# Transposing features per tile, layer blocks of two tiles and a drifting token stream in a recommendation kernel

## The chip, the cores and the metric

The kernel runs on one core of one Trainium2 chip. A core has a matrix engine (TensorE, "PE" in the profile, with its weight loads listed as "PEld"), a vector engine (VectorE, "DVE"), an activation engine (ScalarE, "ACT"), a general engine (GpSimd, "POOL", which here issues the gathers) and a queue engine (SyncE, "SP"). They run their own instruction streams in order and meet at semaphores. The metric is device microseconds of one execution. The profile is a hardware record of one execution.

## The reference

For each of B = 16384 rows the model looks up embeddings, averages them, runs a three-layer perceptron and adds a "wide" sum:

```python
tok = word_emb[token_idx].mean(axis=1)        # 32 rows of 300 out of 50000
e1 = emb_mh1[mh1_idx].mean(axis=1)            # 20 rows of 64; e2, e3 alike
o1 = emb_oh1[oh1_idx]                         # one row of 64; o2, o3, o4 alike
emb = concatenate([tok, e1, e2, e3, o1, o2, o3, o4], axis=1)      # 748 columns
wide = wide_mh1[mh1_idx].sum(axis=(1, 2)) + ... + wide_oh4[oh4_idx][:, 0]
h = relu(emb @ W1 + b1)                       # 1024
h = relu(h @ W2 + b2)                         # 512
h = relu(h @ W3 + b3)                         # 256
return sigmoid(h @ Wd + bd + wide)
```

All arrays are fp32.

## The kernel before

A tile is 128 rows, so there are 128 tiles. Each tile is worked through in 11 steps (`STEPS`; ten of 6 and one of 4 row pairs), and four kinds of work are interleaved in every step, in one order written out by hand (`manual_schedule`, the loop at L476 to L524):

- **Counts.** The seven small tables are looked up by counting. VectorE builds one-hot matrices for the next step (`one_hots`, "row" and "slice", L294), TensorE multiplies them (12 matmuls per step, "pc", L312), and ScalarE copies the result out as fp8 ("cnt", L319). The PSUM tile "pc" has one buffer and the one-hots have two, so the matmuls of step i wait for the copy of step i-1, and VectorE's one-hots for step i+1 wait for the matmuls of step i-1.
- **Tokens.** POOL gathers rows of the word table (`tokens`, L224): a group is two gathers of 128 rows of 300 values, 16 groups make a tile. VectorE adds a group to a running sum (`add_up`, L211 to L215) three groups after its gathers were written into the program (`TOK_LAG`). The pool of row tiles has 6 buffers, so a gather waits until the group six before it has been added. The `Paced` object spreads the 16 groups over the 11 steps, 1 or 2 per step.
- **Small sums.** The counts of the tile before are multiplied with the tables (`small_sums`, "pg", 138 matmuls per tile, L337) and VectorE reduces the result into the feature tile `g` (L343). When a tile is done, `wide_term` (L351) sums the seven wide columns into a 128x1 tile.
- **Layers.** Four finished tiles form a block of 512 columns. `transposed` (L371) turns their features by 24 TensorE transposes ("pt", L378) into six chunks, each of which VectorE scales into the operand `x` (L379). Then `layer` (L388, L397) does W1, W2 and W3 with 88 matmuls of 512 columns per block, each of which stands as two records in the profile, and ScalarE's relu after each output chunk. The last product ("po", L413) also takes the wide tiles in, by one transposing matmul per tile (L417). `Paced` gives each step a share of this work. The last four tiles are blocks of 2, 1 and 1.

In one step VectorE's order is one-hots, token adds, reduce; TensorE's is pc, pg, layer matmuls. `ps_h` has two PSUM buffers, used in turn for transposes, layer outputs, `po` and the transposed lookup keys. After the last counts, 11 more steps follow, in which only small sums and layers are left.

Of the kernel before, what the change touches and what calls it, by code (L numbers as in the profile page):

```python
# [17 lines left out]
P = 128  # L18
# [5 lines left out]
TOK_LAG = 3  # L24
BLOCK = 512
HALF = P // 2
# [3 lines left out]
CHUNK_WORK = 1  # L30
TABLE_PACE = 1.2
LAYER_TIME = 10
# [6 lines left out]
G_COLS = TOK_D + 7 * ROW  # L39
# [7 lines left out]
def kernel(  # L47
# [23 lines left out]
    NSUB = BLOCK // P  # L71
# [5 lines left out]
    for f in SMALL:  # L77
# [4 lines left out]
    tokp = ctx.enter_context(tc.tile_pool(name="tok", bufs=2 * TOK_LAG))  # L82
    const = ctx.enter_context(tc.tile_pool(name="const", bufs=1))
    idxp = ctx.enter_context(tc.tile_pool(name="idx", bufs=2))
# [4 lines left out]
    gp = ctx.enter_context(tc.tile_pool(name="g", bufs=NSUB + 1))  # L89
    wp = ctx.enter_context(tc.tile_pool(name="wide", bufs=2 * NSUB))  # L90
    xp = ctx.enter_context(tc.tile_pool(name="x", bufs=1))
# [8 lines left out]
        [(0, 128)],  # L100
        [(128, 256)],
        [(256, 300), (684, 748)],
        [(300, 428)],
        [(428, 556)],
        [(556, 684)],
    ]
# [7 lines left out]
    scale = const.tile([P, NK], F32, name="scale")  # L114
    nc.vector.memset(scale, 1.0)
    nc.vector.memset(scale[:, 0:2], 1.0 / N_TOK)
    nc.vector.memset(scale[0 : TOK_D - 256, 2:3], 1.0 / N_TOK)
    nc.vector.memset(scale[:, 3:4], 1.0 / N_MH)
    nc.vector.memset(scale[0:EMB, 4:5], 1.0 / N_MH)
# [25 lines left out]
    def load_tables(part0, tag):  # L145
        raw = xp.tile([P, PART, ROW], F32, name="raw", tag=tag)
        for f in SMALL:
            table, (h0, h1) = tables[f], slices[f]
            full, rest = divmod(table.shape[0], P)
            a, b = max(h0, part0), min(h0 + full, part0 + PART)  # L150
            if a < b:
                nc.sync.dma_start(
                    out=raw[:, a - part0 : b - part0, :],
                    in_=table[(a - h0) * P : (b - h0) * P, :].rearrange("(h p) d -> p h d", p=P),
                )
            if rest and part0 <= h0 + full < part0 + PART:
                nc.vector.memset(raw[:, h0 + full - part0, :], 0.0)
                nc.sync.dma_start(out=raw[0:rest, h0 + full - part0, :], in_=table[full * P :, :])
        return raw
# [44 lines left out]
    under_way = []  # L204
    features = {}

    def add_up(t, q, rows):
# [4 lines left out]
        else:  # L212
            nc.vector.tensor_add(tok_sum, tok_sum, a)  # L213
            to = features[t][:, 0:TOK_D] if q == n_groups - 1 else tok_sum
            nc.vector.tensor_add(to, tok_sum, b)  # L215

    def tokens(t, it):


        for q in range(n_groups):  # L220
            rows = tokp.tile([P, TOK_GROUP * TOK_D], F32, name="tok_rows")
            for r in range(TOK_GROUP):
                j = q * TOK_GROUP + r
                nc.gpsimd.indirect_dma_start(  # L224
                    out=rows[:, r * TOK_D : (r + 1) * TOK_D],
                    out_offset=None,
                    in_=word,
                    in_offset=bass.IndirectOffsetOnAxis(ap=it[:, j : j + 1], axis=0),
                )
            under_way.append((t, q, rows))  # L230
            if len(under_way) > TOK_LAG:
                add_up(*under_way.pop(0))
            yield 1

    def last_tokens():
        for group in under_way:
            add_up(*group)

    def load_indices(blk):
# [15 lines left out]
        return it, ix  # L255
# [71 lines left out]
    def small_sums(g, cnt):  # L327
# [3 lines left out]
        for i in (0, 2, 4, 6):  # L331
# [9 lines left out]
            at = TOK_D + i * ROW  # L341
# [9 lines left out]
    def wide_term(g):  # L351
        wide = wp.tile([P, 1], F32, name="wide")
        at = TOK_D + EMB
        nc.vector.tensor_reduce(
            wide,
            g[:, at : at + 6 * ROW].rearrange("p (c d) -> p c d", d=2 * ROW)[:, :, 0:2],
# [3 lines left out]
        nc.vector.tensor_add(wide, wide, g[:, G_COLS - 1 : G_COLS])  # L360
        return wide

    def chunk(g, k):
        if k < 2:
            return g[:, k * P : (k + 1) * P]
        if k == 2:
            return g[:, 2 * P : TOK_D + EMB]
        at = TOK_D + (1 + 2 * (k - 3)) * ROW + 1
        return g[:, at : at + 2 * EMB]

    def transposed(x, gs):  # L371

        n = len(gs) * P
        for k in range(NK):
            kk = chunk_k[k]
            pt = ps_h.tile([P, BLOCK], F32, name="pt", tag="ph")
            for s, g in enumerate(gs):
                nc.tensor.transpose(pt[:kk, s * P : (s + 1) * P], chunk(g, k), ident)  # L378
            nc.vector.tensor_scalar(  # L379
                x[:kk, k, 0:n], pt[:kk, 0:n], scale[:kk, k : k + 1], None, ALU.mult  # L380
            )
            yield CHUNK_WORK

    def layer(dst, weights, bias, src, kks, n_out, n):
        for m in range(n_out):
            ph = ps_h.tile([P, BLOCK], F32, name="ph", tag="ph")
            for k, kk in enumerate(kks):
                nc.tensor.matmul(  # L388
                    ph[:, 0:n],
                    weights[:kk, k, m * P : (m + 1) * P],  # L390
                    src[:kk, k, 0:n],
                    start=(k == 0),
                    stop=(k == len(kks) - 1),
                )
                if k < len(kks) - 1:
                    yield 1
            nc.scalar.activation(dst[:, m, 0:n], ph[:, 0:n], AF.Relu, bias=bias[:, m : m + 1])  # L397
            yield 1

    def mlp(b0, gs, wides):  # L400

        n = len(wides) * P
        x = xp.tile([P, NK, BLOCK], F32, name="x", tag="even")
        yield from transposed(x, gs)
        h1 = xp.tile([P, M1, BLOCK], F32, name="h1", tag="odd")
        yield from layer(h1, w1_sb, b1_sb, x, chunk_k, M1, n)
        h2 = xp.tile([P, M2, BLOCK], F32, name="h2", tag="even")
        yield from layer(h2, w2_sb, b2_sb, h1, [P] * M1, M2, n)
        h3 = xp.tile([P, M3 + 1, BLOCK], F32, name="h3", tag="odd")
        yield from layer(h3, w3_sb, b3_sb, h2, [P] * M2, M3, n)  # L410
        po = ps_h.tile([1, BLOCK], F32, name="po", tag="ph")
        for k in range(M3):
            nc.tensor.matmul(  # L413
                po[:, 0:n], wd_sb[:, k : k + 1], h3[:, k, 0:n], start=(k == 0), stop=False
            )
        for s, wide in enumerate(wides):
            nc.tensor.matmul(  # L417
                po[:, s * P : (s + 1) * P], wide, ident, start=False, stop=(s == len(wides) - 1)
            )
        y = h3[0:1, M3, 0:n]  # L420
        nc.scalar.activation(y, po[:, 0:n], AF.Sigmoid, bias=bd_sb)
# [3 lines left out]
    class Paced:  # L425


        def __init__(self, gen):
            self.gen, self.done = gen, 0

        def to(self, size):
            while self.done < size:
                work = next(self.gen, None)
                if work is None:
                    return
                self.done += work
# [27 lines left out]

    tiles = B // P
    mlp_time = (NK * (CHUNK_WORK + M1) + M1 * M2 + M2 * M3 + M3) * LAYER_TIME
    ctx.enter_context(tc.manual_schedule())
    sizes = [NSUB] * (tiles // NSUB - 1) + [NSUB - 2, 1, 1]
    it, ix = load_indices(0)
# [5 lines left out]
    gs, wides, layers, before, b0 = [], [], None, None, 0  # L475
    for t in range(tiles + 1):  # L476
        s = t % NSUB
        sums = None
        if before:
            features[t - 1] = g = gp.tile([P, G_COLS], F32, name="g")  # L480
            sums = sums_by_step(small_sums(g, before))
        if t < tiles:
            if s == 0 and t:
                it, sc = next_it, next_sc
            cnt = cp.tile([P, 2, HALF, n_h], FP8, name="cnt", tag="counts")
            toks = Paced(tokens(t, it[:, s, :].bitcast(U32)))
        else:
            last_tokens()
        for i in range(STEPS):
            if t < tiles:  # L490
                hot_now = hot
                if s == 1 and i == 0 and t + NSUB < tiles:
                    next_it, ix = load_indices(t // NSUB + 1)
                if s == 2 and i == 0 and t + NSUB < tiles + 1:
                    next_keys = lookup_keys(ix)
                if i < STEPS - 1:
                    hot = one_hots(sc, s, i + 1)
                elif t + 1 < tiles:
                    hot = one_hots(next_sc if s == NSUB - 1 else sc, (s + 1) % NSUB, 0)
                counts(cnt, hot_now, i)  # L500
                tables_on_chip.to(TABLE_PACE * (t * STEPS + i - 2))
                if t == 1 and i == STEPS - 1:
                    load_weights()
                toks.to(n_groups * (i + 1) / STEPS)
            if s == 2 and i == 1 and t + NSUB < tiles + 1:
                next_sc = key_columns(next_keys)
            done = next(sums) if sums else 0
            if layers:
                share = (n_h + layers_time) * (i + 1) / STEPS - done
                layers.to((layers_before + share) / LAYER_TIME)  # L510
        if layers:
            layers_before += layers_time
        if before:
            assert done == n_h and next(sums, None) is None
            gs.append(g)
            wides.append(wide_term(g))
        before = cnt if t < tiles else None
        if len(gs) == sizes[0]:
            if layers:
                layers.finish()  # L520
# [44 lines left out]
```

## Time and profile before

| | |
|---|---|
| median of 9 runs | 7125.86 us (7106.88 to 7139.03) |
| the profiled execution | 7131.99 us, of which the span of its instructions is 7130.2 us |
| TensorE | 5657.8 us busy (79%), 41320 matmul records, mean granted clock 0.905 |
| VectorE | 3793.0 us (53%) |
| ScalarE | 2461.9 us (35%) |
| POOL | 3882.2 us (54%), 4096 gathers of 948 ns |
| DMA engines | 32.9% of their time on gathers |

Busy shares are averages over the whole span. A line of the groups gives busy time, the mean of one instruction, and after the bar the time for which its engine stood idle just before it, with what released it. "issue" is time in which nothing visible was waited for; "remote" and "another core or an unknown queue" mean that a wait ended without a record that explains it. Matmuls are pipelined: in the timeline, "x18" with 4.08 us is a train of 18, and the pitch of one is smaller than the duration of one.

### The profile page before, as it was taken

The numbers are of one execution on the slowest core, as the hardware profiler recorded it, in microseconds if no ns is written. First come the engines' busy times: TensorE is split into PE (matmuls) and PEld (weight loads), VectorE is DVE, ScalarE is ACT, GpSimd is POOL, SyncE is SP. The second block draws the span as 40 slices with busy tenths as digits, with TensorE's granted clock in tenths as the row PEclk, the third lists the DMA queues.
The fourth block names the chain that finished last, engine by engine and source line by source line (L and its number), as shares of the span: only waits on it lengthen the run. The fifth ranks groups of instructions, "written<-read, shape, count | busy, mean of one in ns | idle before, by whom it ended". The sixth has DMA issues, their size and how long they took to land.

```text
span 7130.2 us, 104252 instructions
## 1 busy us (share of the span) xinstructions
PE 5657.8 (79%) x41320; PEld 3481.0 (49%) x41320; DVE 3793.0 (53%) x8014; ACT 2461.9 (35%) x1938; POOL 3882.2 (54%) x4103
## 2 busy tenths in 40 slices
PE   4688788877877888877878877877878787887889
PEld 3444444544444444444444444444444444444457
DVE  6555555555555555555555555555555555555553
ACT  4333333333333333333333333333333333333332
POOL 6555555555555555555555555555555555555552
PEclk8789998999899998898989999998999999999899
DMA  5333333333333333333333333333333333333331
GB/s 155 93 91 90 94 92 92 92 91 92 90 90 92 91 90 92 92 92 90 90 90 94 91 92 91 91 92 90 89 89 92 91 90 90 93 93 90 91 86 46
DMA packets 252890, 652.60 MB, mean 92 GB/s; under 512 B 119009, under 2 KB 119524, under 8 KB 252399
## 3 DMA queue, kind: packets, MB, share of 16 engines
q0 software_dynamic: 196608, 629.41, 32.9%
q1 hardware_dynamic: 55791, 16.53, 1.0%
q8 instruction: 323, 5.29, 0.3%
q14 instruction: 168, 1.38, 0.1%
HBM read 645.59 MB, written 0.07 MB: 91 GB/s over the span
## 4 chain that ended last, share of the span: by engine, by line
PE 37%; another core or an unknown queue 19%; issue 16%; DVE 16%; POOL 6%; ACT 2%; DMA 2%; DVEq 0%; POOLq 0%; ACTq 0%
PE ph L388 17%; PE pg L337 13%; PE pc L312 6%; POOL tok_rows L224 6%; DVE slice L294 5%; DVE own L213 4%; DVE own L215 3%; DMA tok_rows<-in_word_emb_dram,it 2%; DVE row L294 2%; ACT cnt L319 2%; PE pt L378 1%; DVE g L343 1%; DVE x L379 1%; DVE own L211 0%
## 5 line engine op out<-in xcount | busy, mean ns | idle before, releaser
L224 POOL DMA_INDIRECT tok_rows<-in_word_emb_dram,it x4096 | 3881.3, 948 | 3169.5 <-DVE own L215 1726.8
L319 ACT ACTIVATE cnt<-pc 128x1656 fp8e3<-128x1656 f32 (+1 forms) x1408 | 2122.4, 1507 | 3971.4 <-remote 1931.8
L337 PE MATMUL pg<-terms,cnt 128*128 128x195 bf16 x17664 | 2111.5, 269 | 396.6 <-issue 241.5
L337 PEld LDWEIGHTS <-cnt 128*128 128x128 fp8e3 x17664 | 1745.7, 146 | 630.1 <-issue 490.1
L294 DVE TENSOR_TENSOR row<-own,sc 128x768 bf16<-128x768 bf16 (+1 forms) x1408 | 761.5, 541 | 1900.5 <-remote 1248.5
L312 PE MATMUL pc<-slice,row 64*128 64x138 bf16 x16384 | 804.3, 233 | 1001.3 <-ACT cnt L319 418.9
L388 PE MATMUL ph<-x,w_sb 128*128 128x512 f32 (+5 forms) x3264 | 1569.4, 611 | 25.2 <-issue 23.0
L312 PEld LDWEIGHTS <-row 64*128 64x128 bf16 x16384 | 567.0, 99 | 2010.3 <-issue 1495.0
L388 PE MATMUL ph<-h,w_sb 128*128 128x512 f32 (+2 forms) x2720 | 1337.3, 619 | 32.0 <-issue 30.4
L213 DVE TENSOR_TENSOR own<-own,tok_rows 128x300 f32<-128x300 f32 x1920 | 918.3, 478 | 65.8
L343 DVE TENSOR_REDUCE g<-pg 128x130 f32<-128x390 f32 (+1 forms) x512 | 261.2, 510 | 1208.0 <-remote 579.9
L215 DVE TENSOR_TENSOR own<-own,tok_rows 128x300 f32<-128x300 f32 x1792 | 856.9, 478 | 61.9
L388 PEld LDWEIGHTS ph<-x,w_sb 128*128 128x128 f32 (+1 forms) x3264 | 601.6, 206 | 481.6 <-issue 475.9
L294 DVE TENSOR_TENSOR slice<-own,sc 128x828 bf16<-128x828 bf16 (+1 forms) x1408 | 795.4, 565 | 0.0
L388 PEld LDWEIGHTS ph<-h,w_sb 128*128 128x128 f32 x2720 | 508.1, 210 | 426.6 <-issue 424.7
L397 ACT ACTIVATE h<-ph,b_sb 128x512 f32<-128x512 f32 (+2 forms) x476 | 314.7, 661 | 616.9 <-PE ph L388 329.2
L379 DVE TENSOR_SCALAR x<-pt,scale 128x512 f32<-128x512 f32 (+4 forms) x204 | 138.3, 712 | 49.2 <-PE pt L378 45.2
L378 PE MATMUL pt<-ident,g 128*128 128x128 f32 (+1 forms) x768 | 120.2, 304 | 8.1 <-DVE x L379 7.7
L378 PEld LDWEIGHTS pt<-ident,g 128*128 128x128 f32 (+1 forms) x768 | 101.8, 159 | 12.2 <-DVE x L379 10.6
L211 DVE TENSOR_TENSOR own<-tok_rows 128x300 f32<-128x300 f32 x128 | 61.3, 479 | 4.4
L215 DVE TENSOR_TENSOR g<-own,tok_rows 128x300 f32<-128x300 f32 x128 | 60.2, 470 | 4.4
L413 PE MATMUL po<-h,wd_sb 128*1 128x512 f32 (+2 forms) x136 | 60.9, 566 | 0.3
(34 smaller groups left out, 286.4 us busy)
## 6 DMA issues: line engine op xcount, KB each, us to landing
tok_rows<-in_word_emb_dram,it POOLq DMA_INDIRECT x4096
ix<-in_idx_dram SPq DMA_DIRECT2D x128, 32.0 KB
w_sb<-in_W_dram SPq DMA_DIRECT2D x6, 512.0 KB
raw<-in_mh_dram SPq DMA_DIRECT2D x3, 747.5 KB
it<-in_idx_dram SPq DMA_DIRECT2D x32, 64.0 KB
w_sb<-in_W_dram SPq DMA_DIRECT2D x1, 2048.0 KB
raw<-in_mh_dram SPq DMA_DIRECT2D x1, 617.5 KB
out_dram<-h SPq DMA_DIRECT2D x31, 2.0 KB
```

What stands on the lines that cost most here:

```text
L213: nc.vector.tensor_add(tok_sum, tok_sum, a)
L215: nc.vector.tensor_add(to, tok_sum, b)
L224: nc.gpsimd.indirect_dma_start(out=rows[:, r * TOK_D : (r + 1) * TOK_D], out_offset=None, in_=word, in_offset=bass.IndirectOffsetOnAxis(ap ...
L294: nc.vector.tensor_tensor(one[:, 0:rows, :].rearrange("p i (n d) -> p i n d", d=2), iota[:, 0:n].rearrange("p (n d) -> p n d", d=2).unsque ...
L312: nc.tensor.matmul(pc[:, f, k // n, at : at + n_h], hot[0][half, k, :], hot[1][half, k, :], start=True, stop=True,)
L319: nc.scalar.activation(cnt[:, :, b : b + rows, :].rearrange("l f (g k) h -> l f g (k h)", g=2), pc[:, :, :, 0 : n * n_h], AF.Copy, scale=0 ...
L337: nc.tensor.matmul(pg[:, j, :], by_slice[:, :, h], terms[:, h, :], start=(h == h0), stop=(h == h1 - 1))
L343: nc.vector.tensor_reduce(g[:, at : at + n * ROW].rearrange("p (f d) -> p f d", f=n), pg[:, 0:n, :].rearrange("p f (c d) -> p f d c", c=3) ...
L378: nc.tensor.transpose(pt[:kk, s * P : (s + 1) * P], chunk(g, k), ident)
L379: nc.vector.tensor_scalar(x[:kk, k, 0:n], pt[:kk, 0:n], scale[:kk, k : k + 1], None, ALU.mult)
L388: nc.tensor.matmul(ph[:, 0:n], weights[:kk, k, m * P : (m + 1) * P], src[:kk, k, 0:n], start=(k == 0), stop=(k == len(kks) - 1),)
L397: nc.scalar.activation(dst[:, m, 0:n], ph[:, 0:n], AF.Relu, bias=bias[:, m : m + 1])
```

## The change

- Blocks for the layers have two tiles (256 columns), 63 of them and two of one tile. Every array that holds layer data shrinks to 256 columns.
- Features are no longer transposed at the start of a block. A tile's small features are transposed in step 1 after its sums are complete (`add_small`), its token sum two steps after it is complete (`add_tokens`, from its own tile `g_tok`). TensorE does 4 and 3 transposes, VectorE 3 and 2 copies that scale, straight into the block's operand (`x_small`, `x_tok`). In both engines this work stands behind the counts and ahead of the token adds of its step.
- The wide sum is written into a column of `g` and so is transposed with the small features; it becomes a row, `wide_row`, which VectorE adds to `po`. The matmuls of L417 go.
- The rows of W1 are loaded in another order, to suit the chunks.
- The stream of tokens is one for all tiles, and runs over 1408 + 16 steps (`WAKE`): 1.4403 groups a step in place of 1.4545, so that the token sums fall behind the small sums by up to 16 steps towards the end. The row tiles have 8 buffers in place of 6, the index tiles 3 in place of 2.
- The layers' pace is reckoned from when a block is complete to when the next one will be, and a layer's end ends the step's share of layer work (`yield None`).

```diff
+TOK_BUFS = 8
+WAKE = 16
+LAYER_TILES = 2
-LAYER_TIME = 10
+LAYER_TIME = 2.5
-    tokp = ctx.enter_context(tc.tile_pool(name="tok", bufs=2 * TOK_LAG))
+    tokp = ctx.enter_context(tc.tile_pool(name="tok", bufs=TOK_BUFS))
...
+    n_all = B // P * n_groups + TOK_LAG
...
-            to = features[t][:, 0:TOK_D] if q == n_groups - 1 else tok_sum
+            to = tok_sum
+            if q == n_groups - 1:
+                to = sums_of[t] = gp.tile([P, TOK_D], F32, name="g_tok")
...
-        nc.vector.tensor_add(wide, wide, g[:, G_COLS - 1 : G_COLS])
-        return wide
+        nc.vector.tensor_add(g[:, EMB : EMB + 1], wide, g[:, G_COLS - 1 : G_COLS])
...
+        def add_small(self, t, g):
+            at = self.columns(t)
+            pt = ps_h.tile([P, 4, P], F32, name="pt", tag="ph")
+            nc.tensor.transpose(pt[:, 3, :], g[:, 0:P], ident)
+            for k in range(3):
+                c = (1 + 2 * k) * ROW + 1
+                nc.tensor.transpose(pt[:, k, :], g[:, c : c + P], ident)
+            nc.vector.tensor_tensor(
+                self.small[:, 0:3, at], pt[:, 0:3, :], scale.unsqueeze(2).to_broadcast([P, 3, P]), ALU.mult
             )
+            nc.vector.tensor_copy(self.small[0:EMB, 3, at], pt[0:EMB, 3, :])
+            nc.vector.tensor_copy(self.wide[:, at], pt[EMB : EMB + 1, 3, :])
+
+        def add_tokens(self, t, g):
+            if self.tok is None:
+                self.tok = xtp.tile([P, 2, N], F32, name="x_tok")
+            at = self.columns(t)
+            rest = TOK_D - 2 * P
+            pt = ps_h.tile([P, 3, P], F32, name="pt", tag="ph")
+            for k in range(2):
+                nc.tensor.transpose(pt[:, k, :], g[:, k * P : (k + 1) * P], ident)
+            nc.tensor.transpose(pt[0 : EMB + rest, 2, :], g[:, TOK_D - rest - EMB : TOK_D], ident)
+            nc.vector.tensor_single_scalar(self.tok[:, :, at], pt[:, 0:2, :], 1.0 / N_TOK, op=ALU.mult)
+            nc.vector.tensor_single_scalar(
+                self.small[EMB : EMB + rest, 3, at], pt[EMB : EMB + rest, 2, :], 1.0 / N_TOK, op=ALU.mult
+            )
...
-            ph = ps_h.tile([P, BLOCK], F32, name="ph", tag="ph")
+            ph = ps_h.tile([P, N], F32, name="ph", tag="ph")
...
-        for s, wide in enumerate(wides):
-            nc.tensor.matmul(
-                po[:, s * P : (s + 1) * P], wide, ident, start=False, stop=(s == len(wides) - 1)
-            )
         y = h3[0:1, M3, 0:n]
-        nc.scalar.activation(y, po[:, 0:n], AF.Sigmoid, bias=bd_sb)
+        nc.vector.tensor_add(y, po[:, 0:n], block.wide[:, 0:n])
+        nc.scalar.activation(y, y, AF.Sigmoid, bias=bd_sb)
...
+    n_steps = tiles * STEPS + WAKE
+    sizes = [LAYER_TILES] * (tiles // LAYER_TILES - 1) + [1] * LAYER_TILES
...
+    for step in range(n_steps):
+        t, i = divmod(step, STEPS)
+        s = t % NSUB
+        if i == 0:
+            if g is not None:
+                wide_term(g)
+                waiting.append((step + 1, Block.add_small, t - 2, g))
...
+            counts(cnt, hot_now, i)
...
+        if waiting and step >= waiting[0][0]:
+            block = transpose(*waiting.pop(0)[1:])
+            if block:
+                if layers:
+                    layers.finish()
+                layers = Paced(mlp(block), LAYER_TIME * block.n / P)
+                last = block.first + block.n // P
+                begin, left = step, (ready(ends[last] - 1) if last < tiles else n_steps) - step
+        known = set(sums_of)
+        toks.to(n_all * (step + 1) / n_steps)
+        for k in set(sums_of) - known:
+            waiting.append((step + 2, Block.add_tokens, k, sums_of.pop(k)))
...
+        if layers:
+            layers.to(mlp_work * layers.size * (step + 1 - begin) / left + ahead)
     layers.finish()
+    for _, *what in waiting:
+        block = transpose(*what)
+    Paced(mlp(block)).finish()
```

## The prediction

> **What bounds the kernel now.** I read the page's busy shares and chain first, then the groups, then a stretch of the timeline, then the same windows for different stages.
>
> ```profile
> PE 5657.8 (79%) x41320; PEld 3481.0 (49%) x41320; DVE 3793.0 (53%) x8014; ACT 2461.9 (35%) x1938; POOL 3882.2 (54%) x4103
> PE 37%; another core or an unknown queue 19%; issue 16%; DVE 16%; POOL 6%; ACT 2%; DMA 2%; DVEq 0%; POOLq 0%; ACTq 0%
> L224 POOL DMA_INDIRECT tok_rows<-in_word_emb_dram,it x4096 | 3881.3, 948 | 3169.5 <-DVE own L215 1726.8
> L319 ACT ACTIVATE cnt<-pc 128x1656 fp8e3<-128x1656 f32 (+1 forms) x1408 | 2122.4, 1507 | 3971.4 <-remote 1931.8
> L379 DVE TENSOR_SCALAR x<-pt,scale 128x512 f32<-128x512 f32 (+4 forms) x204 | 138.3, 712 | 49.2 <-PE pt L378 45.2
> L378 PE MATMUL pt<-ident,g 128*128 128x128 f32 (+1 forms) x768 | 120.2, 304 | 8.1 <-DVE x L379 7.7
> ```
>
> No engine is full. The chain is TensorE for 37% only; 19% has no named releaser. The table of waits puts 1931.8 us, in 361 waits, on ScalarE's "cnt" for such a "remote" event, and 1726.8 us on POOL for VectorE's token adds. The timeline shows how they hang together:
>
> ```profile
> 3042.99 0.55 PE L312 MATMUL pc<-slice,row 64*128 64x138 bf16 x12
> 3045.16 0.95 POOL L224 DMA_INDIRECT tok_rows<-in_word_emb_dram,it  x1 [0.31 <-issue]
> 3046.30 0.30 PE L337 MATMUL pg<-terms,cnt 128*128 128x195 bf16 x1 [0.46 <-issue]
> 3047.66 0.95 POOL L224 DMA_INDIRECT tok_rows<-in_word_emb_dram,it  x1 [0.30 <-issue]
> 3050.64 1.55 ACT L319 ACTIVATE cnt<-pc 128x1656 fp8e3<-128x1656 f32 x1 [8.51 <-remote]
> 3050.64 0.56 DVE L294 TENSOR_TENSOR row<-own,sc 128x768 bf16<-128x768 bf16 x1 [6.95 <-remote]
> 3052.25 0.87 PE L312 MATMUL pc<-slice,row 64*128 64x138 bf16 x12 [3.13 <-DVE own L213]
> 3052.99 0.94 POOL L224 DMA_INDIRECT tok_rows<-in_word_emb_dram,it  x1 [4.39 <-DVE own L215]
> ```
>
> TensorE's pc ended at 3043.54, yet ScalarE and VectorE, which both wait for it, go on only at 3050.64. Until 3048.61 POOL issued ten gathers without a gap, and TensorE's matmuls came with "issue" holes. Two microseconds after POOL ran out of free row tiles everything went on; VectorE's one-hots and adds then took 2.35 us until POOL had a buffer (3052.99). So a step is not bound by any engine's work but by a cycle: a run of gathers, TensorE's completions seen late, POOL blocked, restart. How the run delays the completion no view says. The windows, with the pc matmuls alone, show that the cycle hardly cares for TensorE's work (columns: time, busy time and count on PE and PEld, clock, DMA):
>
> ```profile
> 110.00:270.00 160.00, 23.54 (x376) 17.63 (x378) 0.70 0.35 94
> 1000.00:2000.00 1000.00, 113.12 (x2348) 79.68 (x2343) 0.91 0.34 92
> 2000.00:4000.00 2000.00, 224.48 (x4644) 157.90 (x4644) 0.91 0.34 91
> 6900.00:7000.00 100.00, 9.53 (x208) 6.27 (x208) 1.00 0.31 84
> ```
>
> At 128 matmuls per 11 steps these are 4.95 us a step before any layer exists, 4.96 and 5.01 with layers, and 5.6 near the end, where a block of four has to be done in 22 steps and TensorE is busy throughout. In time: 1408 steps end near 7064, and 66 us follow, in which nothing is gathered.
>
> **The change, part by part.** The sum is made against the profiled execution, 7131.99 us, which lies 6.1 us above the median.
>
> *Drift, main part.* 1424 steps spread 2051 slots of groups, so when the counts end 2028 are through: 20 groups, 40 gathers fewer stand beside counts. One gather costs 7053 / 4096 = 1.72 us there (the counts run from about 11 to 7064), if the cycle is set by gathers, which the even 4.95 to 5.01 speaks for: -69. If steps cost what they cost whatever they gather, it is 0.
>
> *Drift, tail.* After the last counts 16 steps follow. POOL is up to 5 groups ahead, so at least 15 groups remain (30 x 1.25 us = 38); at the pace of 5.0 us a step it would be 80. I take the gather rate, 2.88 gathers x 1.25 us a step, 58, as VectorE has no one-hots left to wait with. Then come the last tile's transposes, copies and layers, which took 7104.4 to 7128.2 before, with output 26. 84 in place of 66: +18 (ends -2 and +40).
>
> *Eight row tiles.* POOL's waits are for VectorE's adds, not for landings: at each block it is as far ahead as the buffers let it. Two more groups move that point, not the rate at which adds free tiles: 0. What covers this is the cycle; if VectorE ever waited for a landing it would be a gain.
>
> *Blocks of 256.* 5456 records of 512 columns become twice as many of 256.
>
> ```profile
> 6988.36 4.48 PE L388 MATMUL ph<-h,w_sb 128*128 128x512 f32 x10
> 7031.84 4.08 PE L388 MATMUL ph<-x,w_sb 128*128 128x256 f32 x18
> ```
>
> Less the last one's own length (0.62, 0.39), the pitch is 0.429 and 0.217 us: a pair costs 5 ns more, 27 us in all, hidden by TensorE's idle 21%; without that cover it would be +27. But records rise from 41320 to 46772 (+13%), and it is in the dense stretches that completions are late. The price from below: nothing. From the nearest rows: 361 late waits growing by 13% are +255. Between tiles with and without layers, 0.05 us a step for ten more pairs of instructions and all the layer work: 8 more pairs are about 0.025 to 0.04, 35 to 55. This is the nearest row, so +35.
>
> The Trainium skill ("TensorE: Matmul & The Clock Gate", section "Back-to-back issue gap") has a rule against this edit: sustained spacing is about 81 ns at 128 columns and 131 at 512, so that narrow matmuls pay more for each column. Read between its ends, 256 would cost about 98 ns, a pair 65 ns more, and 5456 pairs would be an estimated +355 us of TensorE. The pitches of this trace say 5 ns, and the trace decides.
>
> *Relus* double: 910 of 473 ns (or 367) for 476 of 661, +113 us of ScalarE, hidden by its 65% idle; in front of a "cnt" they are shorter than before. 0, at most +113.
>
> *Transposes.* Gone are 24 transposes and 6 copies in a row at each block's start; in the chain they hold 1% each, 143 us. New are 7 transposes and 5 copies per tile; TensorE's part is the same (896 for 768). VectorE's copies: 384 columns between the rows 480 (256) and 742 ns (512), 0.61; 256 columns 0.48; three narrow ones 0.35 each (the 128-column row): 2.14 us, 274 for 138, and 65 adds to `po`, 31. VectorE is 47% idle and covers that. I take half the 143 back, -71 (ends 0 and -143), since the new work is in the chain too.
>
> *The new waits.* In two steps of eleven VectorE now waits for pc and the transposes of the same step with the token adds behind it, and POOL behind those. The nearest row is the reduce L343, which waits for TensorE likewise: 512 of them, 1208.0 us of idle VectorE, 2.36 each, but only 1% of the chain, 0.14 each. 256 new ones: +36 by the chain; +604 if all idle time counted; below nothing if such a pause breaks a run of gathers. I take +36, since POOL is mostly blocked or has freed tiles in hand. `ps_h` now turns between transposes and layer groups, so a group may wait for the relu before it: about 0.7 us on TensorE, in its idle time, 0.
>
> *Wide sums.* 256 records (33.5 us) go, 0 to -33: 0. *Even blocks:* the 31 steps from 6889 to 7064 lose their excess of about 0.6 us: -19, of which I take -15, since the single-tile blocks remain. *Loads and indices:* as many as before, by SP.
>
> Sum: -69 + 18 + 35 - 71 + 36 - 15 = -66. From 7132 that is 7066, and by the median 7060.
>
> **Rivals.** *Later completions (slower).* The late waits follow the number of TensorE's instructions: 361 become 408, 47 x 5.35 us = +251 in place of +35, so 7060 + 216 = 7276. For it: late completions come between dense matmuls, while the 33 us from 6954, with 512-column matmuls for two thirds of each step, have no "remote" wait. Against: 4.95 us a step without any layer. It decides from about 13 further waits. *POOL behind the transposes (slower).* Half of the 604 us counts: 7060 - 36 + 302 = 7326. Against: the reduces do the same today for 1% of the chain. *Broken runs (faster).* A pause of VectorE stops POOL for a moment and completions come through; if one tenth of the 1931.8 us goes, with no term for instructions, 7060 - 193 - 35 = 6832. *No change.* Steps cost the same however much they gather, all else as taken: 7060 + 69 = 7129. For it: the first steps, with other work, took 4.95 us too.
>
> **Numbers.** Chances: the sum as taken 0.45 (its own range 6980 to 7110), later completions 0.23, behind the transposes 0.12, broken runs 0.10, no change 0.10. The range from 6840 to 7340 leaves out about half of the broken runs and a third of the two slower ones. A measurement of this kernel can tell 0.2%, 14 us. Faster: 0.45 + 0.10 less a little, 0.53; within 0.2%: 0.09; slower: 0.38.
>
> **What would show it.** Right: pc windows at about 4.95 us a step from 1000 to 6000; the last gather some 30 us before the end; no change in the count of "remote" waits at cnt; copies out of pt with idle time ahead, but under 2% of the chain. Wrong: "remote" time at cnt well over 1932 us (first rival), POOL's wait for adds well over 1727 us behind copies (second), both well under (third). The prediction fails if the price of more instructions, or of a pause in VectorE, is not what today's rows say.

## The result and the profile after

The changed kernel takes 7529.5 us (median of 10 runs, 7527.1 to 7559.0) where the kernel before takes 7130.2 (31 runs): 1.0575 times as long, 95% interval 1.0559 to 1.0591. That is slower by 400 us, and above the range. In some later sessions almost no completion of TensorE came late, and there the same two kernels take 5266.0 and 5192.0 us, ratio 0.986 (0.9843 to 0.9876), so that the change is faster by 74 us. I call the first condition "late" and the second "clean"; every run below stands beside runs of the kernel before on the same chip in the same session.

The profiled execution of the comparison has a span of 7543.2 us. The page's busy shares, chain and groups, of the changed kernel (a group's line: busy time, mean ns, then the idle time before it and what ended it):

```profile
PE 5913.9 (78%) x46772; PEld 4676.1 (62%) x46772; DVE 3907.4 (52%) x8513; ACT 2572.1 (34%) x2403; POOL 3887.3 (52%) x4103
...
PE 53%; another core or an unknown queue 20%; DVE 12%; issue 10%; ACT 6%; DMA 0%; DVEq 0%; SPq 0%; ACTq 0%
...
L232 POOL DMA_INDIRECT tok_rows<-in_word_emb_dram,it x4096 | 3886.4, 949 | 3609.2 <-DVE own L220 2303.5
...
L324 ACT ACTIVATE cnt<-pc 128x1656 fp8e3<-128x1656 f32 (+1 forms) x1408 | 2122.2, 1507 | 3139.5 <-remote 1516.2
...
L299 DVE TENSOR_TENSOR row<-own,sc 128x768 bf16<-128x768 bf16 (+1 forms) x1408 | 762.2, 541 | 1742.8 <-remote 1285.7
...
L428 ACT ACTIVATE h<-ph,b_sb 128x256 f32<-128x256 f32 (+1 forms) x910 | 426.6, 469 | 1740.4 <-remote 776.0
```

The relus of the kernel before, to be set against the last line:

```profile
L397 ACT ACTIVATE h<-ph,b_sb 128x512 f32<-128x512 f32 (+2 forms) x476 | 314.7, 661 | 616.9 <-PE ph L388 329.2 <-remote 178.6 <-PE pc L312 99.9
```

"remote" at cnt fell from 1931.8 to 1516.2 us, but at the relus it rose from 178.6 to 776.0. Together that is 2292 in place of 2110 us. So the first rival's mark, more "remote" time at cnt, did not come. POOL's wait for token adds rose from 1726.8 to 2303.5 us, the mark that the second rival had announced. The time is spread over the whole run, as the windows with the pc matmuls alone show (busy time and count on PE and PEld, clock, DMA):

```profile
110.00:270.00 160.00, 19.19 (x348) 13.84 (x347) 0.79 0.33 89
1000.00:2000.00 1000.00, 111.68 (x2188) 77.11 (x2188) 0.87 0.32 85
2000.00:4000.00 2000.00, 216.73 (x4400) 151.42 (x4400) 0.88 0.32 85
4000.00:6000.00 2000.00, 223.86 (x4524) 155.27 (x4524) 0.89 0.33 88
```

At 128 matmuls per 11 steps these are 5.32, 5.29 and 5.14 us a step from 1000 to 6000, where before had 4.96 and 5.01. A stretch of the timeline of the changed kernel shows what became of the cycle:

```profile
2988.81 0.95 POOL L232 DMA_INDIRECT tok_rows<-in_word_emb_dram,it  x1 [0.30 <-issue]
...
2989.25 0.47 ACT L428 ACTIVATE h<-ph,b_sb 128x256 f32<-128x256 f32 x1 [5.30 <-remote]
...
2992.18 1.55 ACT L324 ACTIVATE cnt<-pc 128x1656 fp8e3<-128x1656 f32 x1 [2.46 <-remote]
...
2992.34 0.56 DVE L348 TENSOR_REDUCE g<-pg 128x130 f32<-128x390 f32 x1 [6.16 <-remote]
...
2993.29 0.58 DVE L299 TENSOR_TENSOR slice<-own,sc 128x828 bf16<-128x828 bf16 x1
...
2995.74 0.56 DVE L388 TENSOR_TENSOR x_small<-pt,scale 128x384 f32<-128x384 f32 x1 [1.87 <-PE pt L387]
...
2997.59 0.41 DVE L448 TENSOR_TENSOR h<-po,wide_row 1x256 f32<-1x256 f32 x1 [0.80 <-issue]
...
2997.93 0.46 DVE L216 TENSOR_TENSOR own<-own,tok_rows 128x300 f32<-128x300 f32 x1
...
2999.17 0.95 POOL L232 DMA_INDIRECT tok_rows<-in_word_emb_dram,it  x1 [9.42 <-DVE own L220]
```

A run of gathers ends at 2989.76. The late completion comes through at 2992.18 to 2992.34, about 2.5 us later, much as in the kernel before. But VectorE then has more to do ahead of the token adds: it waits 1.87 us for the transposes, copies three times, and waits 0.80 us for `po`. The add begins at 2997.93, and POOL has stood for 9.42 us. In the stretch shown of before, POOL restarted 2.35 us after the late completion; here it takes 6.8. This is one of the long stops and not the usual one: over the whole run the median restart takes 2.35 us in both kernels, but POOL stands for more than 6 us 91 times in the changed kernel (680 us) and 20 times in the kernel before (125 us; counted in the traces).

The mean time from a step's first pc matmul to the next one's, by position in the tile (counted in the traces, tiles 8 to 114; the last column is their sum; the third row is the run e3_late_c below, with the copies behind the token adds):

```
step of the tile    0    1    2    3    4    5    6    7    8    9   10     tile
before           4.49 5.43 5.28 5.54 5.11 5.56 5.69 4.47 5.27 4.39 3.85    55.08
changed          5.62 6.79 4.09 7.30 5.87 4.63 5.30 5.07 4.74 4.78 3.76    57.95
copies behind    6.18 6.90 4.40 5.60 5.15 5.31 4.99 4.97 5.40 4.43 3.71    57.04
```

The changed kernel loses around step 1, where the small features are transposed, and the steps up to 4 (+3.8 us); the rest of the tile gives back 1.0. With the copies behind the adds the long step 3 goes.

### The profile page after: what moved, and what is told of

It is laid out like the page before. It is cut to its first block, busy times and chain, and to the rows that moved or that the text cites. A ratio compares the mean times of both kernels' runs of the same rounds, so it can differ in the third digit from the quotient of the medians.

```text
span 7543.2 us, 116204 instructions
## 1 busy us (share of the span) xinstructions
PE 5913.9 (78%) x46772; PEld 4676.1 (62%) x46772; DVE 3907.4 (52%) x8513; ACT 2572.1 (34%) x2403; POOL 3887.3 (52%) x4103
## 4 chain that ended last, share of the span: by engine, by line
PE 53%; another core or an unknown queue 20%; DVE 12%; issue 10%; ACT 6%; DMA 0%; DVEq 0%; SPq 0%; ACTq 0%
PE ph L419 24%; PE pg L342 17%; PE pc L317 8%; ACT cnt L324 5%; DVE own L216 4%; DVE slice L299 3%; DVE own L220 3%; PE po L444 1%; ACT h L428 1%; PE pt L387 1%; DVE row L299 1%; PE pt L403 1%; DVE g L348 0%; PE pt L384 0%
## 5 line engine op out<-in xcount | busy, mean ns | idle before, releaser
L232 POOL DMA_INDIRECT tok_rows<-in_word_emb_dram,it x4096 | 3886.4, 949 | 3609.2 <-DVE own L220 2303.5
L324 ACT ACTIVATE cnt<-pc 128x1656 fp8e3<-128x1656 f32 (+1 forms) x1408 | 2122.2, 1507 | 3139.5 <-remote 1516.2
L342 PE MATMUL pg<-terms,cnt 128*128 128x195 bf16 x17664 | 2170.7, 273 | 399.9 <-issue 343.8
L299 DVE TENSOR_TENSOR row<-own,sc 128x768 bf16<-128x768 bf16 (+1 forms) x1408 | 762.2, 541 | 1742.8 <-remote 1285.7
L419 PE MATMUL ph<-h,w_sb 128*128 128x256 f32 (+1 forms) x5200 | 1382.1, 409 | 60.5 <-issue 55.2
L419 PE MATMUL ph<-x_small,w_sb 128*128 128x256 f32 (+3 forms) x4160 | 1192.0, 414 | 85.9 <-issue 64.1
L419 PEld LDWEIGHTS ph<-h,w_sb 128*128 128x128 f32 x5200 | 1017.4, 209 | 230.7 <-issue 101.3
L428 ACT ACTIVATE h<-ph,b_sb 128x256 f32<-128x256 f32 (+1 forms) x910 | 426.6, 469 | 1740.4 <-remote 776.0
L419 PEld LDWEIGHTS ph<-x_small,w_sb 128*128 128x128 f32 (+1 forms) x4160 | 821.4, 211 | 235.0 <-issue 117.7
L419 PE MATMUL ph<-x_tok,w_sb 128*128 128x256 f32 (+1 forms) x2080 | 618.2, 404 | 12.8 <-issue 12.7
L419 PEld LDWEIGHTS ph<-x_tok,w_sb 128*128 128x128 f32 x2080 | 405.3, 207 | 74.3 <-issue 25.3
L388 DVE TENSOR_TENSOR x_small<-pt,scale 128x384 f32<-128x384 f32 x128 | 70.9, 554 | 119.8 <-PE pt L387 89.2
L444 PE MATMUL po<-h,wd_sb 128*1 128x256 f32 (+1 forms) x260 | 87.8, 464 | 41.9 <-ACT h L428 35.0
```

The costliest lines, as they stand in the source:

```text
L232: nc.gpsimd.indirect_dma_start(out=rows[:, r * TOK_D : (r + 1) * TOK_D], out_offset=None, in_=word, in_offset=bass.IndirectOffsetOnAxis(ap ...
L299: nc.vector.tensor_tensor(one[:, 0:rows, :].rearrange("p i (n d) -> p i n d", d=2), iota[:, 0:n].rearrange("p (n d) -> p n d", d=2).unsque ...
L324: nc.scalar.activation(cnt[:, :, b : b + rows, :].rearrange("l f (g k) h -> l f g (k h)", g=2), pc[:, :, :, 0 : n * n_h], AF.Copy, scale=0 ...
L342: nc.tensor.matmul(pg[:, j, :], by_slice[:, :, h], terms[:, h, :], start=(h == h0), stop=(h == h1 - 1))
L419: nc.tensor.matmul(ph[:, 0:n], weights[: src.shape[0], k, m * P : (m + 1) * P], src, start=(k == 0), stop=(k == len(srcs) - 1),)
L444: nc.tensor.matmul(po[:, 0:n], wd_sb[:, k : k + 1], h3[:, k, 0:n], start=(k == 0), stop=(k == M3 - 1))
```

## Experiments

Differences in the late condition are given as the time above the kernel before of the same session; the changed kernel itself is 400 above. They are single executions unless a range is given, and the kernel before spreads over 7098 to 7147 us there, so I read nothing into less than about 30 us. The first four kernels (e1, e3, e4 and e5) met the clean condition, while their expectations assume the late one.

**Is the loss in the late completions?**

> The changed kernel once more, beside the kernel before on the same chip. In the first four runs the kernel before took 5261 us and no completion of TensorE was late, where it had taken 7130 us in the comparison on record. Theory 'late completions' (the whole loss of 5.8% is late completions, which this place does not have): where the kernel before takes about 5261 us the changed kernel takes 5200 to 5250 us, so faster; where it takes about 7130, 7530 again. Theory 'VectorE's new waits or longer runs': slower by some per cent in both places, 5400 us or more beside 5261.

> The kernel before, unchanged, for its profile. If it takes about 5261 us: TensorE busy 95% or more at a clock of 0.99, 'remote' waits at cnt under 20 us in place of 1931.8, and POOL waiting mainly for nothing but its own issue. If about 7130 us: the rows shown before.

Measured: 5192.03 us (5191.26 to 5193.04) beside 5266.01. The pages of the kernel before and of the changed kernel there, busy shares and chain, and the group of cnt of the kernel before:

```profile
PE 5088.0 (97%) x41320; PEld 3161.2 (60%) x41320; DVE 3763.7 (71%) x8014; ACT 2445.6 (46%) x1938; POOL 3892.2 (74%) x4103
...
PE 30%; DMA 26%; DVE 17%; issue 16%; POOL 11%; ACT 0%; DVEq 0%; SPq 0%; POOLq 0%; ACTq 0%
...
L319 ACT ACTIVATE cnt<-pc 128x1656 fp8e3<-128x1656 f32 (+1 forms) x1408 | 2120.7, 1506 | 2053.4 <-PE pc L312 2042.2
```

```profile
PE 5072.6 (98%) x46772; PEld 4161.1 (80%) x46772; DVE 3906.8 (75%) x8513; ACT 2594.8 (50%) x2403; POOL 3891.1 (75%) x4103
...
PE 93%; DVE 3%; issue 2%; DMA 2%; POOL 1%; ACT 0%; SPq 0%; DVEq 0%; ACTq 0%; POOLq 0%
```

ScalarE's copies are as long as in the late condition (cnt 1506 for 1507 ns), and "remote" is gone. That is not only a matter of missing records: counted in the traces, cnt starts more than 2 us after both the end of its last pc matmul and ScalarE's own previous instruction in 372 of 1408 steps of the kernel before when late, in 315 of the changed kernel, and in none of either when clean. TensorE is now nearly always busy: 97% before, 98% after. It is the whole bound of the changed kernel, with 93% of the chain; in the kernel before the chain also runs through the gathers' landings (DMA 26%) and VectorE. So the loss appears only where completions come late; without them the change does gain.

**Are the gathers their cause?** One gather of each group is left out, and its rows are added twice:

```diff
-        a, b = rows[:, 0:TOK_D], rows[:, TOK_D : 2 * TOK_D]
+        a = b = rows[:, 0:TOK_D]
-                for r in range(TOK_GROUP):
+                for r in range(1):
```

> The kernel before with one gather in place of two for each group; VectorE adds the gathered rows twice, so its work is the same, but half of the token rows are left out. Theory 'late completions are caused by the back-to-back gathers': where the kernel before takes about 7130 us it falls to 5250 to 5600 us, with few 'remote' waits at cnt; where it takes about 5265 us (no late completions, TensorE 97% busy) it stays at 5250 to 5270. Theory 'a slower TensorE or clock on the first chip': it stays above 6900 us beside 7130.

Measured: 5155.24 us beside 7101.95, late condition. The busy shares of its page:

```profile
PE 5056.1 (98%) x41320; PEld 3140.3 (61%) x41320; DVE 3795.5 (74%) x8014; ACT 2447.7 (47%) x1938; POOL 1936.0 (38%) x2055
```

With half of the gathers the kernel is bound by TensorE at a granted clock of 0.997, in the session in which the kernel before took 7101.95. So in the late condition the full stream of gathers is needed to make completions late; it is not enough, since the clean condition has it too. The clock of 0.88 to 0.91 in the late runs does not explain them: 0.905 in place of 0.99 is 9%, as an estimate the most that it could add to a kernel bound by TensorE, and the kernel before takes 35% longer.

**More TensorE instructions, more relus?** The kernel before with the matmuls split (e1), and with the relus split as well (e7, for which the last two lines stand, inside the loop over the parts):

```diff
-            for k, kk in enumerate(kks):
+            cuts = [slice(c, min(n, c + 2 * P)) for c in range(0, n, 2 * P)]
+            for part in cuts:
+                for k, kk in enumerate(kks):
...
-                    ph[:, 0:n],
+                        ph[:, part],
...
-            nc.scalar.activation(dst[:, m, 0:n], ph[:, 0:n], AF.Relu, bias=bias[:, m : m + 1])
+                nc.scalar.activation(dst[:, m, part], ph[:, part], AF.Relu, bias=bias[:, m : m + 1])
```

> The kernel before (7130 us), with each layer matmul of 512 columns issued as two of 256 columns into the two halves of the same PSUM tile; relus, transposes, token stream and pacing as before. Theory 'more instructions' (TensorE's completions come late when many short matmuls run beside gathers): most of the loss comes back here, 7400 to 7560 us, pc windows at 5.2 to 5.35 us a step. Theory 'VectorE's new waits' and theory 'longer runs with 8 row tiles': 7100 to 7170 us, since neither is touched. My forecast's own term for it was +35 us: 7165.

Clean: 5262.98 us beside 5261.40, ratio 1.0002 (0.9992 to 1.0012); the repetition e1_split_b 5276.62 beside 5273.52, also clean. TensorE's busy time is 5090.7 us with the matmuls split (e1_split) and 5088.0 us without (the profile above).

> The kernel before with each layer matmul as two of 256 columns, and the relus left at 512, a third time. Where completions come late (kernel before about 7130): theory 'more TensorE instructions' 7400 to 7500, as with the relus split too; theory 'more hand-overs between TensorE and ScalarE' 7100 to 7200. Where nothing comes late: within 5 us of the kernel before, as twice already.

> The kernel before with each layer matmul and each relu of 512 columns issued as two of 256: all of the instructions that blocks of 256 add. Theory 'more instructions': beside 7130 us of the kernel before 7400 to 7600; beside about 5265 us, where nothing comes late, within 10 us of it. Theory 'the loss has nothing to do with the count of instructions': 7100 to 7170 beside 7130.

Late: 7365.91 beside 7145.15 (+221) for the matmuls alone, 7465.83 beside 7101.95 (+364) with the relus. The +221 lies between both expectations and nearer to "instructions". The table of waits (us in total, times, longest) for the matmuls alone, then with the relus:

```profile
ACT cnt L319 <- remote: 2455.3, 412, 12.9
...
ACT h L399 <- remote: 238.8, 39, 8.5
```

```profile
ACT cnt L319 <- remote: 1490.7, 308, 12.7
...
ACT h L399 <- remote: 503.3, 104, 9.8
...
PE ph L390 <- ACT h L399: 666.9, 250, 11.1
```

For the matmuls alone, the "remote" waits of cnt rise from 361 to 412, 14%, for 13% more records. That they follow the records in proportion is not shown: counted from the recorded ends of pc, as above, the steps in which cnt is over 2 us late rise from 372 to 387 and those over 1 us late from 420 to 505.

With the relus split, "remote" at cnt falls again and TensorE waits 667 us for relus. This wait comes from the way the split is written. The two halves lie in one PSUM tile, and in all 434 pairs of full blocks the second half's first matmul began only after the first half's relu had ended. The changed kernel has a tile for each relu: there 27% of the layer groups begin after the end of the relu before, and the same wait is 6.4 us. So the further 143 us of e7 cannot be taken as the price of the changed kernel's relus.

**The place of the copies.** In the changed kernel, the block that issues transposes and copies is moved behind the token adds of its step. The end of the block of layers before, with its `po` add, is issued there too and moves along:

```diff
-        if waiting and step >= waiting[0][0]:
-            block = transpose(*waiting.pop(0)[1:])
...
         toks.to(n_all * (step + 1) / n_steps)
...
+        if waiting and step >= waiting[0][0]:
+            block = transpose(*waiting.pop(0)[1:])
```

> The changed kernel (7529.5 us), with the transposes of a tile and their copies put behind the token adds of their step instead of ahead of them, so that POOL no longer waits behind a copy. Theory 'VectorE's new waits': at least half of the loss goes, 7330 us or less, and POOL's wait for adds falls from 2303 us toward 1750. Theory 'more instructions' and theory 'longer runs': 7490 to 7560 us.

Clean: 5222.63 (ratio 0.9925, 0.9908 to 0.9941), and e3_late_b 5225.14: 31 us worse than the changed kernel's 5192.

> The changed kernel with transposes and copies behind the token adds, a third time. Where completions come late: theory 'VectorE's new waits' 7330 or less beside 7130; otherwise 7490 to 7600. Where nothing comes late: 5220 to 5228, as twice already.

Late: 7412.14 beside 7145.15, +267 in place of +400. That is a third of the loss, between the two expectations. POOL's and VectorE's rows of the waits:

```profile
POOL tok_rows L232 <- DVE own L220: 2178.8, 728, 16.2
...
DVE row L299 <- remote: 1028.7, 216, 8.9
```

In the changed kernel these were 2303.5 and 1285.7. POOL's stops (idle time ahead of a gather) in the late condition, counted in the traces, show how the edits differ:

```
                               over 1 us       of these over 6 us
before                       587, 2053 us          20, 125 us
matmuls split (e1_split_c)   686, 2320 us          11,  72 us
relus split too (e7_relus)   728, 2404 us          17, 131 us
changed                      607, 2516 us          91, 680 us
copies behind (e3_late_c)    669, 2387 us          14, 119 us
```

The stops grow about as the times do (+267, +351, +463 and +334 us, beside +221, +364, +400 and +267). Split matmuls give more stops of the usual length; the changed kernel has longer ones, and with the copies behind the adds the long ones are gone again. So the same edit costs in one condition and pays in the other.

**The drift.** The token stream paced over 1408 steps again, in two places:

```diff
-        toks.to(n_all * (step + 1) / n_steps)
+        toks.to(n_all * (step + 1) / (tiles * STEPS))
```

> The changed kernel (7529.5 us) with the token stream paced over the 1408 counting steps, as before (1.455 groups a step), with 16 steps still behind them: the drift alone is undone. By my forecast's terms (drift -69 and +18) it costs 51 us more: 7580. If steps cost what they cost whatever they gather: about 7530, less up to 40 of gathers that no longer stand in the tail: 7490 to 7530.

Clean: 5250.77 (0.9979, 0.997 to 0.9989), so the drift is worth 59 us there against the changed kernel's 5192.

> The changed kernel without the drift once more. Where nothing comes late it cost 59 us (5251 beside 5192). Where completions come late (kernel before about 7130): if a step is set by its gathers, about 7530 + 50 = 7580; if a step costs what it costs whatever it gathers, 7490 to 7530.

Late: 7616.02 beside 7132.07, +484: the drift is worth about 85 us.

**Row tiles.** The changed kernel with 6, and with 4:

```diff
-TOK_BUFS = 8
+TOK_BUFS = 6
```

> The changed kernel (7529.5 us) with 6 row tiles in place of 8. Theory 'longer runs' (with 8 tiles a run of gathers lasts longer, and late completions come from long runs): half of the loss or more goes, 7330 us or less. Theory 'more instructions' and theory 'VectorE's new waits': 7500 to 7570 us. My forecast priced the tiles at 0.

Clean: 5191.47, no difference.

> The changed kernel with 6 row tiles in place of 8, once more. Where nothing comes late it cost nothing (5191 beside 5192). Where completions come late (kernel before about 7130): theory 'the row tiles are worth their 120 us between 4 and 8': 7560 to 7620, so that three-tile blocks with 6 row tiles (7566) gained little by themselves; theory 'more instructions in proportion' needs 7750 or more here, since two thirds of the extra matmuls gone should be worth about 150 to 240 us.

> The changed kernel with 4 row tiles in place of 8: a run of gathers is at most 8 long from any stop of VectorE. Theory 'long runs of gathers make completions late': beside 7130 us of the kernel before, 7300 or less in place of 7530. Theory 'density of both streams, whatever the length of runs': 7450 to 7600. Where nothing comes late: 5192 or, if VectorE now waits for landings, up to 5400.

Late: 7666.30 beside 7137.53 (+529) with 6, and 7649.95 beside 7132.07 (+518) with 4. The eight tiles thus save about 120 to 130 us in the changed kernel, and shorter runs of gathers do not cure the loss: "long runs" falls. How they save it was not examined.

**Blocks of three tiles**, then the same with the copies behind the adds as in e3:

```diff
-TOK_BUFS = 8
-LAYER_TILES = 2
+TOK_BUFS = 6
+LAYER_TILES = 3
...
-    xsp = ctx.enter_context(tc.tile_pool(name="x_small", bufs=3))
+    xsp = ctx.enter_context(tc.tile_pool(name="x_small", bufs=2))
...
-    sizes = [LAYER_TILES] * (tiles // LAYER_TILES - 1) + [1] * LAYER_TILES
+    sizes = [LAYER_TILES] * (tiles // LAYER_TILES - 1) + [2] + [1] * LAYER_TILES
```

> The changed kernel with blocks of three tiles (384 columns, 42 blocks of three or two and three of one) in place of two, which needs 6 row tiles, 2 operand buffers: of the 5456 matmul records that blocks of 256 add, about two thirds go. Theory 'more instructions' (splitting the kernel before in this way cost 364 us beside 7102): beside about 7130 us of the kernel before, 7530 - 240 = 7290, between 7230 and 7350. Where nothing comes late (kernel before about 5265): within 20 us of the changed kernel's 5192. Theory 'the loss is in the transposes and their waits': about 7530 beside 7130.

> Blocks of three tiles with 6 row tiles, and transposes and copies behind the token adds. Where completions come late: if the place of the copies is worth here what it was with blocks of two (7412 in place of 7530), 7566 - 118 = 7450; if the two undo the same loss, 7540 to 7580. Where nothing comes late: 5192 + 31 = 5223 for the place of the copies, and 0 to 10 less for fewer instructions.

Late: 7565.78 beside 7132.07 (+434), and 7274.19 beside 7137.53 (+137). The first was a miss when set against the changed kernel, but against its own base, 6 row tiles (+529), larger blocks give about 95 us. With the copies behind the adds another 297 go, far more than the 133 with blocks of two. Whether the larger blocks or the 6 row tiles make that difference is open, since blocks of two with 6 row tiles and the copies behind were not run. What is left is +137, 1.9%. POOL's row of the waits there, to be set against 2303.5 in the changed kernel:

```profile
POOL tok_rows L232 <- DVE own L220: 2050.8, 727, 15.9
```

**PSUM shared with the transposes.** Transposes in a bank of their own, layer groups in turn in the halves of the other:

```diff
-            pt = ps_h.tile([P, 4, P], F32, name="pt", tag="ph")
+            pt = ps_h.tile([P, 4, P], F32, name="pt", tag="pt", bufs=1)
...
-            ph = ps_h.tile([P, N], F32, name="ph", tag="ph")
+            ph = half()
```

> The changed kernel with a PSUM bank of its own for the transposes, and the two halves of the other bank in turn for the layers' outputs: transposes and layer groups no longer wait for one another. My forecast priced this contention at 0. If it is 0: within 30 us of 7530 beside 7130, or within 5 us of 5192 beside about 5265. If the contention makes the loss: 7400 or less beside 7130.

Measured, clean: 5725.59 beside 5273.52. Inconclusive for its question, for the two halves acted as one buffer: 583 of 910 layer groups waited for the relu before them (waits of PEld and PE).

```profile
PEld ph L425 <- ACT h L434: 603.7, 583, 1.6
...
PE ph L425 <- ACT h L434: 375.6, 579, 1.2
```

Beside the changed kernel's 5192 the edit loses over 500 us, with one buffer for layer groups and one for transposes. What sharing the buffers costs stays open.

No kernel tried that does all of the work beats the kernel before in the late condition; in the clean one the changed kernel is the best, level with its form with 6 row tiles.

## Why the prediction was wrong, step by step

- **The reading of the bound was right.** The cycle of gather runs, late completions and restarts was the bound, and thinning the gathers ended it. What I did not see is that it need not be there: in the clean condition TensorE is 97% busy. That the change gains 74 us there, close to the 66 of my sum, is chance: the sum was made from rows of the late condition.
- **Blocks of 256, +35: this step failed most.** Of two rows I took the step time with and without layers as the nearer, over the growth of the late waits (+255). The matmuls alone cost +221, more than six times the term. "4.95 us a step before any layer exists" was the wrong witness: equal step times did not mean that instructions cost nothing, and that window also had a clock of 0.70 beside 0.91 later. (The "ten more pairs" there are ten instructions, five matmul records with their weight loads, and the "8" are eight; the ratio stands.) The 412 waits come close to the 408 of the other row, but by the second count above that agreement is partly luck. The 27 us of pitch do not show: split matmuls cost 1.6 and 3.1 us in the clean condition.
- The Trainium skill's rule on that point ("TensorE: Matmul & The Clock Gate", section "Back-to-back issue gap") gave an estimate of +355 us of TensorE for narrow matmuls. In the clean condition TensorE's busy time grew by 2.7 us and the kernel's time by 1.6 and 3.1 us, so the trace's pitch was right and the estimate does not hold for these fp32 matmuls.
- **Relus, 0 with an end of +113: not settled.** The changed kernel's relus meet late completions more often (139 "remote" waits, 776.0 us, for 70 and 178.6), which the term left out. What that costs is open: the 143 us of e7 contain a wait for relus that the changed kernel does not have.
- **The new waits, +36: mis-sized.** Moving the copies and the `po` add behind the adds gains 133 us with blocks of two and 297 with blocks of three. I priced a wait by the reduces' share of the chain, 0.14 us each. But the reduces stand behind the token adds, and the new copies stand ahead of them: after a late completion what VectorE has ahead of the adds lengthens the stop of POOL, and the 91 stops of over 6 us become 14 when it is moved. The `po` add, which I counted as 31 us of work, is among it; its own part was not measured.
- **Eight row tiles, 0: failed in size.** In the changed kernel they gain about 125 us in the late condition, 0 in the clean one. I argued that more tiles move the point at which POOL stops and not the rate.
- **Drift, -69 and +18, so -51: right in sign and nearly in size**, 85 us late and 59 clean. The tail alone was larger than priced: the counts' last copy starts at 7437.1, so 106 us follow, where I had 84 (106 was the upper end I gave, at the pace of 5.0 us a step), and the last gather comes 47 us before the end, not 30.
- **Transposes in the chain, -71, wide sums, even blocks:** not tried by themselves. If the parts measured are simply added (221 for the matmuls, 133 for the place of the copies, -85 for the drift, -125 for the row tiles), they give +144 of the +400. They come from different kernels and need not add, as the two results on the copies show. The remainder, over half of the loss, is not assigned; the relus and the transposes in PSUM are the parts without a price.
- **The rivals.** "Later completions" (7276) had nearly the right price for the matmuls (+251, and e1_split_c shows +221 by itself), but its mark did not come in the changed kernel (cnt 1516.2 us, under 1932). "POOL behind the transposes" (7326) had the right mark. I weighed them one against the other, with the smaller terms of the forecast under each. They happened together, and my range ended just above the second.

## What to carry to other kernels

When the profile shows waits that no record explains, price an edit by how often it makes some engine meet such a wait (instructions of the late engine, hand-overs to the engine that waits) and by what stands between the late event and the restart of the stalled queue, not by busy time. Work put ahead of the operation that frees a blocked queue can lengthen every restart, even on an engine that is half idle. An experiment that splits an operation can bring a wait of its own, so look at its table of waits before its time is taken as a price. And ask whether the disturbance belongs to the kernel or to the session: here the verdicts on the change and on the place of the copies turned round between two sessions, and an edit that is free in one cost 221 us in the other.

## What the runs showed of the hardware that was not expected

- The same program took 5261 to 5274 us in three sessions and 7102 to 7145 in four others beside the recorded comparison. Both conditions were met on a chip listed under one number (0). What selects them is not known; I did not find it in the trace.
- Gathers and DMA packets are equally long in both (gathers 948 and 950 ns; a packet of 4800 bytes of the word table takes 185 ns at the median in both, counted in the traces). But the semaphore updates recorded for the gathers' completions differ: 25,016 in the late profile of the kernel before and 65,413 in the clean one, where 16 for each of 4096 gathers would be 65,536. The path of semaphore updates is a suspect, but the profile does not tell late updates from lost records: in e6_thin, where nothing is late, 27,713 of 32,768 are on record.
- In the stretch of the changed kernel from which lines are shown above, between 2986.4 and 2989.3, TensorE issues about one small-sum matmul in 0.7 us, with "issue" holes, where a train just before had one in 0.1. Instruction loads do not explain the late completions: of the 372 steps with cnt over 2 us late in the kernel before, 137 have an instruction load in the wait or within 2 us ahead of it, and the same stretches moved by 7 to 187 us have one in 148 to 204 cases.
